# Graph layer and mixture of experts on one core: carries joined two tiles at a time without masks, and a bias add moved from GpSimd to VectorE

## The chip, the cores and the metric

The kernel runs on one core of a Trainium2 chip. The metric is device time in microseconds (us). A core has five engines that each work through their own instructions in order: TensorE (PE in the profile, its weight loads PEld), VectorE (DVE), ScalarE (ACT), GpSimd (POOL) and SyncE (SP). They meet through semaphores. DMA transfers are issued from the queues of SP, of ScalarE and of GpSimd.

## The reference, cut to what matters

There are 6250 nodes with 256 features and 100,000 edges with 96 features. The edges come sorted by `dst`, the node that they end in.

```python
out1 = segment_sum(edge_attr, dst)            # sum of the edges of each node
cnt  = segment_sum(ones, dst)
out2 = where(cnt > 0, segment_max(edge_attr, dst), 0)
out3 = out1 / maximum(cnt, 1)
h = concatenate([xn, out1, out2, out3, u], axis=1)     # xn = layernorm(x)
x = x + relu(h @ W1 + b1) @ W2 + b2 + xn
...
x = x + layernorm(xm + top2_experts(xm)) * gamma + beta   # xm = layernorm(x)
```

The change touches `out1` and `out2`, and the place where `b2` is added. The second layer (16 experts, two for each node) is not touched.

## The kernel before, in words

**Tiles and groups.** The nodes are cut into NT = 50 tiles of P = 125. Groups g0 to g12 take them from the last tile to the first: g0 has 2 tiles, every other group 4. The kernel has an MLP stage (about the first 820 us), which goes through the groups, and then a stage of expert blocks. An edge stream runs inside the MLP stage.

**Edge stream.** For most edges sums and maxima are made by VectorE in `steps` (L299 to L330): edges are cut into runs, and each run is scanned from its end to its start, so that the row of an edge holds the sum and the maximum over the rest of its node's edges in that run. A step for one edge of every run is a pair of instructions of 125x768 elements (L316 and L317, then L319 and L320), with loads (L176) and stores to `rows_d` (L329) through SP's queue. A node whose edges go on past the end of a run needs the rest from the following run. `chain_runs` (L378) works this out for all runs of a region and stores it as rows of `carry_d` (L440, GpSimd's queue). There are seven regions, each of which has to be there before the groups that need it.

**From edges to a group's input.** For groups g2 to g12:
- `index_nodes` (L621), called four times for several groups at once, finds for each node the row of `rows_d` with its first edge (`first_i`) and the row of `carry_d` with its possible carry (`next_i`). The mask `cross` is 1 where the node has a carry and 0 where not; `gate_m` is plus or minus the largest float, from the same mask.
- `take_edges` (L718) and `take_carry` (L726) fetch the rows with indirect DMAs that GpSimd issues, one for each tile.
- `join_edges` (L733) adds the carry times `cross` to the sum (L735), and takes the maximum with the carry cut down by `gate_m` (L737). Both are VectorE instructions of 96 elements, for each tile.
- `mask_edges` (L740, ScalarE) clears nodes without edges and makes the mean. `turn` (L745) transposes on PE and copies on ScalarE.

Groups g0 and g1 get their edges in another way (windows) and have no joins.

**The node's own features.** `take_x` loads `xt`; `stats_x`, `root_x`, `scale_x` find the layernorm. `keep_x` (L709) turns `xt` into x plus its layernorm, with four ScalarE instructions of 256 elements (L714), and then GpSimd adds `b2`, spread over the partitions as `b2b`, to all four tiles in one instruction (L716). When the MLP has its output, `residual` (L782, VectorE) adds it to `xt` (L784) and makes the next statistics. That add also frees the accumulator that the matmuls of the following group use (L766, L771).

**After the MLP.** `norm_b` (L801, ScalarE, L806) writes the normed row `xr`, `turn_b`, `logits`, `choose` (L829), `rank` and `place` (L864) find the two experts, and `send` (L889) stores two rows for each node to `xg_d` with GpSimd's indirect DMAs (L891). `xr` has one buffer, so the next group's `norm_b` waits for these stores.

**The order of the work** is written out by a planner at build time. Each task has a slot; group g begins at slot B = 12 g, and each engine gets its instructions in the order of the tasks. Between one slot and the next the planner puts pieces of the edge stream into VectorE's order, as long as a credit lasts: a slot of a full group gives 4.6 (us, as the planner sees it), a piece (a pair of instructions) takes 1.9, and tasks on VectorE take their own `cost`. What a slot overdraws is missing in the next. If `take_edges` needs a region that isn't finished, the stream is emitted up to it at once (`edges_until`, L1165).

Of group g, `scale_x` is in slot B-10, `take_edges` in B-10 and B-9, `take_carry` in B-9 and B-8, `keep_x` in B-7, the joins of tiles 0 and 1 in B-6 and of tiles 2 and 3 in B-5, `mask_edges` in B-5 and B-4, `residual` in B+9 to B+12. Between them lie those of other groups: in B-9 `norm_b` of group g-2 and `norm_x` of g, in B-8 and B-7 `turn_b` of g-2, in B-5 `choose` of g-2, in B-2 `place` of g-2. (For g2, `keep_x` and the first joins share slot B-4.)

```python
at_slot(B - (4 if g == GW else 7), keep_x, g)
...
for i in range(n if g >= GW else 0):
    at_slot(B - (4 if g == GW else 6) + i // 2, join_edges, g, i, cost=0.6)
    at_slot(B - (4 if g == GW else 5) + i // 2, mask_edges, g, i)
```

Of the kernel before, what the change touches and what calls it, by code (L numbers as in the profile page):

```python
# [9 lines left out]
F32 = mybir.dt.float32  # L10
# [4 lines left out]
OP = mybir.AluOpType  # L15
# [4 lines left out]
P = 125  # L20
PA = 80
RR = 8
GW = 2
WE = 20
WB = 5
JR = (6, 5, 5, 10, 21, 20, 28)
# [13 lines left out]
BIG = 3.4028234663852886e38  # L40
# [4 lines left out]
def kernel(  # L45
# [18 lines left out]
    nc = tc.nc  # L64
    N, D = x.shape
    E, EF = edge.shape
# [3 lines left out]
    NT = N // P  # L70
    EJ = E // P
    EP = P * RR
# [17 lines left out]
    GRP = [(GS * (NG - 1 - g), GS * (NG - 1 - g) + (GS if g else N0)) for g in range(NG)]  # L90
# [5 lines left out]
    dram = ctx.enter_context(tc.tile_pool(name="dram", bufs=1, space=DRAM))  # L96

    rows_d = dram.tile([ER, 2 * EF], F32, name="rows_d")
    carry_d = dram.tile([len(JR) * EP, 2 * EF], F32, name="carry_d")
    xg_d = dram.tile([NE * N, DR], F32, name="xg_d")  # L100
    y_d = dram.tile([NE * N, D], I32, name="y_d")

# [26 lines left out]
    meta = ctx.enter_context(tc.tile_pool(name="meta", bufs=1))  # L129
    ne_n = meta.tile([P, NT], F32, name="ne_n")  # L130
    rc_n = meta.tile([P, NT], F32, name="rc_n")
    cross = meta.tile([P, NT], F32, name="cross")
    gate_m = meta.tile([P, NT], F32, name="gate_m")
    first_i = meta.tile([P, NT], I32, name="first_i")
    next_i = meta.tile([P, NT], I32, name="next_i")
    cnt_f = meta.tile([P, NT], F32, name="cnt_f")
# [14 lines left out]
    b2b = wgt.tile([P, D], F32, name="b2b")  # L151
# [34 lines left out]

    mlp = ExitStack()
    ld = mlp.enter_context(tc.tile_pool(name="ld", bufs=2))
    ga = mlp.enter_context(tc.tile_pool(name="ga", bufs=4))
    wk = mlp.enter_context(tc.tile_pool(name="wk", bufs=2))  # L190
    htp = mlp.enter_context(tc.tile_pool(name="ht", bufs=HC + 1))
    gtp = mlp.enter_context(tc.tile_pool(name="gt", bufs=2))
# [185 lines left out]
    def chain_runs(c):  # L378
        prev = prevs.pop(c)
        ct = chp.tile([P, RR, 2 * EF], F32, name="ct")  # L380
        kb, kp, kb2 = (chp.tile([P, RR], F32, name=nm) for nm in ("kbar", "kp", "kbar2"))

        def over_runs():

            nc.vector.tensor_scalar(kb, kall[:, c], 2.0, -1.0, op0=OP.mult, op1=OP.add)
            nc.vector.tensor_scalar(kb, kb, BIG, None, op0=OP.mult)
            nc.vector.tensor_tensor_scan(kp[:, ::-1], kall[:, c, ::-1], kall[:, c, ::-1], 1.0, op0=OP.mult, op1=OP.min)
            nc.vector.tensor_scalar(kb2, kp, 2.0, -1.0, op0=OP.mult, op1=OP.add)
            nc.vector.tensor_scalar(kb2, kb2, BIG, None, op0=OP.mult)
            run = tuple(a[:, RR - 1, :] for a in prev)  # L390
            for h in range(2):
                nc.scalar.copy(ct[:, RR - 1, h * EF:(h + 1) * EF], run[h])
            for r in reversed(range(RR - 1)):
                to = ct[:, r, 0:EF], ct[:, r, EF:]
                nc.vector.scalar_tensor_tensor(to[0], run[0], kall[:, c, r:r + 1], prev[0][:, r, :], op0=OP.mult, op1=OP.add)
                nc.vector.scalar_tensor_tensor(to[1], run[1], kb[:, r:r + 1], prev[1][:, r, :], op0=OP.min, op1=OP.max)
                run = to
                if r % 3 == 0:
                    yield 1.8
            for_pe(to_features)  # L400

        def to_features():
            over_runs.pk = pk = eps.tile([EF, 3, P], F32, name="ps")
            nc.tensor.transpose(pk[:, 0, :], kp[:, 0:1].to_broadcast([P, EF]), ident[:P, :P])
            for h in range(2):
                nc.tensor.transpose(pk[:, 1 + h, :], ct[:, 0, h * EF:(h + 1) * EF], ident[:P, :P])

        def over_partitions():
            pk = over_runs.pk
            st = chp.tile([EF, 2, P + 1], F32, name="st", bufs=2)  # L410
            for h in range(2):
                if chain[0] is None:
                    nc.vector.memset(st[:, h, P:], 0.0)
                else:
                    nc.vector.tensor_copy(st[:, h, P:], chain[0][:, h, 0:1])
            kk = chp.tile([EF, 2, P], F32, name="kk")
            nc.vector.tensor_copy(kk[:, 0, :], pk[:, 0, :])
            nc.vector.tensor_scalar(kk[:, 1, :], kk[:, 0, :], 2.0, -1.0, op0=OP.mult, op1=OP.add)
            nc.vector.tensor_scalar(kk[:, 1, :], kk[:, 1, :], BIG, None, op0=OP.mult)
            for h in range(2):  # L420
                nc.vector.tensor_tensor_scan(st[:, h, P - 1::-1], kk[:, h, ::-1], pk[:, 1 + h, ::-1], st[:, h, P:],
                                             op0=(OP.mult, OP.min)[h], op1=(OP.add, OP.max)[h])
            chain[0] = st
            yield 2.0
            for_pe(to_partitions)

        def to_partitions():
            over_runs.pc = pc = eps.tile([P, 2 * EF], F32, name="ps")
            for h in range(2):
                nc.tensor.transpose(pc[:, h * EF:(h + 1) * EF], chain[0][:, h, 1:], ident[:EF, :EF])  # L430

        def to_runs():
            tmp = chp.tile([P, RR, EF], F32, name="tmp")
            for h, k, o0, o1 in ((0, kp, OP.mult, OP.add), (1, kb2, OP.min, OP.max)):
                cs = ct[:, :, h * EF:(h + 1) * EF]
                nc.vector.tensor_tensor(tmp, over_runs.pc[:, None, h * EF:(h + 1) * EF].to_broadcast([P, RR, EF]),
                                        k[:, :, None].to_broadcast([P, RR, EF]), op=o0)
                nc.vector.tensor_tensor(cs, cs, tmp, op=o1)
                yield 1.9
            nc.gpsimd.dma_start(carry_d[EP * c:EP * (c + 1)].rearrange("(p r) f -> p r f", p=P), ct)  # L440

        return [over_runs, over_partitions, to_runs]

# [36 lines left out]
    def node_cols(b):  # L480
        g0 = sum(IB[:b])
        return GRP[g0 + IB[b] - 1][0], GRP[g0][1]
# [138 lines left out]
    def index_nodes(b):  # L621
# [31 lines left out]
        nc.vector.tensor_mul(m, q, J)  # L653
        nc.vector.tensor_add(m, m, e0)
        nc.vector.scalar_tensor_tensor(cross[:, cols], end, nf, m, op0=OP.mult, op1=OP.is_gt)
        nc.vector.tensor_scalar(gate_m[:, cols], cross[:, cols], 2.0, -1.0, op0=OP.mult, op1=OP.add)
        nc.vector.tensor_scalar(gate_m[:, cols], gate_m[:, cols], BIG, None, op0=OP.mult)

        nc.vector.tensor_scalar(m, q, float(EP), -2.0 * EP, op0=OP.is_equal, op1=OP.mult)
        nc.vector.tensor_add(q, q, m)  # L660
        nc.vector.tensor_add(q, q, q0)
        nc.vector.tensor_scalar(next_i[:, cols], q, nf, 0.0, op0=OP.mult, op1=OP.max)

        nc.vector.scalar_tensor_tensor(m, e0, -2.0, f, op0=OP.mult, op1=OP.add)
        nc.vector.scalar_tensor_tensor(m, J, float(-EP), m, op0=OP.mult, op1=OP.add)
# [43 lines left out]
    def keep_x(g):  # L709

        n = GRP[g][1] - GRP[g][0]
        xt = G[g]["xt"]
        for i in range(n):
            nc.scalar.activation(xt[:, i, :], xt[:, i, :], AF.Identity, scale=G[g]["rs1"][:, i:i + 1],  # L714
                                 bias=G[g]["nb"][:, i:i + 1])
        nc.gpsimd.tensor_tensor(xt[:, :n], xt[:, :n], b2b[:, None, :].to_broadcast([P, n, D]), op=OP.add)  # L716

    def take_edges(c, g, i):  # L718
        t = GRP[g][0] + i
# [5 lines left out]

    def take_carry(c, g, i):  # L726
        t = GRP[g][0] + i
        cg = ga.tile([P, 2 * EF], F32, name="cg")
        nc.gpsimd.indirect_dma_start(out=cg, out_offset=None, in_=carry_d[0:EP * (c + 1), :],
                                     in_offset=IndirectOffsetOnAxis(ap=next_i[:, t:t + 1], axis=0))  # L730
        G[g].setdefault("cg", []).append(cg)

    def join_edges(g, i):  # L733
        t, gi, cg = GRP[g][0] + i, G[g]["at"][:, i, 0:2 * EF], G[g]["cg"][i]
        nc.vector.scalar_tensor_tensor(gi[:, 0:EF], cg[:, 0:EF], cross[:, t:t + 1], gi[:, 0:EF],  # L735
                                       op0=OP.mult, op1=OP.add)
        nc.vector.scalar_tensor_tensor(gi[:, EF:], cg[:, EF:], gate_m[:, t:t + 1], gi[:, EF:],  # L737
                                       op0=OP.min, op1=OP.max)

    def mask_edges(g, i):  # L740
        t, gi = GRP[g][0] + i, G[g]["at"][:, i, 0:2 * EF]
# [417 lines left out]
    def at_slot(T, fn, *a, cost=0.0):  # L1159
        tasks.append((T, len(tasks), fn, a, cost))  # L1160
# [21 lines left out]
    for g, (a, z) in enumerate(GRP):  # L1182
        B, n = SLOTS * g, z - a
        if g:
# [9 lines left out]
            for i in range(n):  # L1194
# [4 lines left out]
                else:  # L1199
# [4 lines left out]
                    at_slot(2 * i + 2, add_window, g, i, cost=0.9)  # L1204
                    at_slot(2 * i + 2, mask_window, g, i, cost=0.4)
                    at_slot(min(2 * i + 5, SLOTS - 2), mean_window, g, i)
            at_slot(B - (4 if g == GW else 7), keep_x, g)
            for k in range(DC):
                at_slot(B - (4 if g == GW else 6) + k, turn, g, k)
            for i in range(n if g >= GW else 0):  # L1210
                at_slot(B - (4 if g == GW else 6) + i // 2, join_edges, g, i, cost=0.6)
                at_slot(B - (4 if g == GW else 5) + i // 2, mask_edges, g, i)
            for k in range(DC, KC + 1):
                at_slot(B - 3 + k - DC + (1 if g == GW and k < DC + 2 else 0), turn, g, k)
# [73 lines left out]
    def loads_3():  # L1288
        nc.sync.dma_start(b2b, bass.AP(tensor=b2.tensor, offset=b2.offset, ap=[[0, P], [1, D]]))
        nc.sync.dma_start(gws, gate_w.rearrange("(k p) e -> p k e", p=128))  # L1290
        nc.sync.dma_start(gbs, bass.AP(tensor=gate_b.tensor, offset=gate_b.offset, ap=[[0, P], [1, NE]]))
# [79 lines left out]
    with tc.manual_schedule():  # L1371
# [21 lines left out]
        root_x(1)  # L1393
        scale_x(1)
        loads_3()
        for t in reversed(range(*node_cols(GW))):
            find_block(t)
        for k in range(DC):
# [94 lines left out]
```

## Time and profile before

| what | us |
|---|---|
| three runs: lowest, median, highest | 1313.06, 1313.23, 1322.8 |
| the profiled execution, its own time | 1304.08 |
| span of that execution | 1302.3 |
| busy: PE, PEld | 1134.1 (87% of the span), 788.7 (61%) |
| busy: DVE, ACT, POOL | 929.0 (71%), 646.4 (50%), 591.3 (45%) |
| GpSimd's bias add (L716), 12 of 4 tiles | 30.0 |
| joins (L735 and L737), 44 of each | 22.7 and 15.7 |

How to read it: "busy" is the time in which an engine had an instruction at work; times are of one execution, and start points are counted from the start of the span. A group in the profile has its line in the code, its engine and operation, what it writes and reads, and the shape of both, then how often it ran, the busy time, the mean duration in ns, and, after the second bar, the idle time of the engine just before it and what ended that. In a timeline the columns are start, duration, engine, line and the instruction; a bracket at the end holds the idle time before it and its releaser. In the list of waits the columns are the total in us, how often, and the longest. The slices are 40 equal parts of the span, each digit the busy share in tenths, and PEclk the TensorE clock that was granted, in tenths of full speed.

### The profile page before, as it was taken

The numbers are of one execution on the slowest core, as the hardware profiler recorded it, in microseconds if no ns is written. First come the engines' busy times: TensorE is split into PE (matmuls) and PEld (weight loads), VectorE is DVE, ScalarE is ACT, GpSimd is POOL, SyncE is SP. The second block draws the span as 40 slices with busy tenths as digits, with TensorE's granted clock in tenths as the row PEclk, the third lists the DMA queues.
The fourth block names the chain that finished last, engine by engine and source line by source line (L and its number), as shares of the span: only waits on it lengthen the run. The fifth ranks groups of instructions, "written<-read, shape, count | busy, mean of one in ns | idle before, by whom it ended". The sixth has DMA issues, their size and how long they took to land.

```text
span 1302.3 us, 16684 instructions
## 1 busy us (share of the span) xinstructions
PE 1134.1 (87%) x4631; PEld 788.7 (61%) x4631; DVE 929.0 (71%) x2465; ACT 646.4 (50%) x1484; POOL 591.3 (45%) x731
## 2 busy tenths in 40 slices
PE   2494899879888879999999999997999999999992
PEld 1262365536545444646465565886888888888882
DVE  4569888869996989989999441444347767776764
ACT  3394256444637452533435333221266766676663
POOL 4122254563466654383643450303046656555664
PEclk9897799889998989989989999998999999999997
DMA  5948876795888897879988311222366777878771
GB/s 161 217 103 237 212 231 183 202 273 149 237 213 260 230 289 192 245 202 257 262 245 241 105 50 62 65 66 81 120 230 223 257 253 262 278 246 270 268 271 70
DMA packets 179473, 260.99 MB, mean 200 GB/s; under 512 B 35915, under 2 KB 145963, under 8 KB 173729
## 3 DMA queue, kind: packets, MB, share of 16 engines
q1 hardware_dynamic: 140241, 202.11, 52.0%
q0 software_dynamic: 39008, 57.22, 15.5%
q8 instruction: 40, 0.66, 0.2%
q14 instruction: 72, 0.59, 0.1%
q10 hardware_dynamic: 112, 0.41, 0.1%
HBM read 146.59 MB, written 121.88 MB: 206 GB/s over the span
## 4 chain that ended last, share of the span: by engine, by line
PE 30%; DMA 8%; DVE 7%; issue 3%; ACT 3%; SPq 2%; POOL 2%; DVEq 0%; POOLq 0%; ACTq 0%
PE acc L1122 9%; PE acc L1142 9%; PE acc L771 6%; DMA eb<-in_eb_dram 5%; PE acc L779 3%; POOL xg_d L891 1%; DMA xt<-in_x_dram 1%; DVE yb L1053 1%; PE pT L1036 1%; ACT yb L1055 1%; DMA rows_d<-rw 1%; DVE bsc L1079 1%; DMA cg<-carry_d,next_i 1%; DVE z L1089 1%; ACT hb L1128 1%
## 5 line engine op out<-in xcount | busy, mean ns | idle before, releaser
L771 PE MATMUL acc<-inT,w1x 128*128 128x500 f32 (+1 forms) x832 | 374.3, 601 | 0.0
L771 PEld LDWEIGHTS acc<-inT,w1x 128*128 128x128 f32 x832 | 162.7, 203 | 184.1 <-issue 182.2
L891 POOL DMA_INDIRECT xg_d<-xr,pos_i x100 | 133.4, 1334 | 241.1 <-DVE xr L886 177.6
L1122 PE MATMUL acc<-xT,wt 128*128 128x256 f32 x912 | 223.9, 389 | 15.2 <-ACT hb L1128 13.6
L1142 PE MATMUL acc<-wt,hb 128*128 128x256 f32 x912 | 206.8, 380 | 0.0
L1122 PEld LDWEIGHTS acc<-xT,wt 128*128 128x128 f32 x912 | 169.8, 192 | 45.9 <-ACT hb L1128 23.0
L1142 PEld LDWEIGHTS acc<-wt,hb 128*128 128x128 f32 x912 | 173.9, 191 | 23.9
L779 PE MATMUL acc<-w2s,hT 128*125 128x256 f32 x800 | 183.6, 386 | 0.0
L773 ACT ACTIVATE hT<-acc,c 128x500 f32<-128x500 f32 (+1 forms) x104 | 68.5, 658 | 226.2 <-PE acc L771 226.0
L779 PEld LDWEIGHTS acc<-w2s,hT 128*125 128x125 f32 x800 | 150.7, 192 | 22.8 <-issue 0.9
L1096 POOL DMA_INDIRECT out_dram<-g,to_i x86 | 95.7, 1113 | 104.2 <-ACT xT L1039 73.0
L1066 POOL DMA_INDIRECT g<-y_d,from_i x86 | 89.9, 1046 | 88.4 <-DVE to_i L1046 51.8
L495 POOL DMA_INDIRECT gb<-in_dst_dram,blk_i x50 | 67.9, 1359 | 131.1 <-DVE blk_i L492 77.6
L1128 ACT ACTIVATE hb<-acc,wt 128x256 f32<-128x256 f32 x200 | 87.9, 465 | 51.7 <-PE acc L1122 51.7
L1055 ACT ACTIVATE yb<-yb,xb 128x256 f32<-128x256 f32 x114 | 51.7, 501 | 103.1 <-DVE yb L1053 101.7
L316 DVE TENSOR_TENSOR rw<-rw,keep 125x768 f32<-125x768 f32 x81 | 77.2, 953 | 11.3 <-DMA rows_d<-rw 9.8
L319 DVE TENSOR_TENSOR rw<-rw,raw 125x768 f32<-125x768 f32 x88 | 83.4, 948 | 0.3 <-DMA raw<-in_edge_dram 0.3
L320 DVE TENSOR_TENSOR rw<-rw,raw 125x768 f32<-125x768 f32 x88 | 83.6, 950 | 0.0
L317 DVE TENSOR_TENSOR rw<-rw,bar 125x768 f32<-125x768 f32 x81 | 82.1, 1013 | 0.0
L756 ACT COPY inT<-pT 128x500 f32<-128x500 f32 (+1 forms) x65 | 35.9, 553 | 89.6 <-PE pT L755 89.5
L722 POOL DMA_INDIRECT at<-rows_d,first_i x44 | 62.5, 1420 | 37.6 <-issue 19.0
L1041 DVE TENSOR_TENSOR xe<-xb,eb 128x512 f32<-128x512 f32 x57 | 39.4, 691 | 55.7 <-DMA eb<-in_eb_dram 55.7
(301 smaller groups left out, 1633.5 us busy)
## 6 DMA issues: line engine op xcount, KB each, us to landing
wt<-in_wpack_dram SPq DMA_DIRECT2D x44, 1026.0 KB
rows_d<-rw SPq DMA_DIRECT2D x46, 960.0 KB
rows_d<-rw SPq DMA_DIRECT2D x46, 540.0 KB
raw<-in_edge_dram SPq DMA_DIRECT2D x46, 480.0 KB
xb<-xg_d SPq DMA_DIRECT2D x57, 261.0 KB
y_d<-yb SPq DMA_DIRECT2D x57, 256.0 KB
raw<-in_edge_dram SPq DMA_DIRECT2D x46, 270.0 KB
xt<-in_x_dram SPq DMA_DIRECT2D x12, 500.0 KB
```

What stands on the lines that cost most here:

```text
L316: nc.vector.tensor_tensor(su, prev[0], keep[c][:, :, s + j, None].to_broadcast(bcast), op=OP.mult)
L317: nc.vector.tensor_tensor(mx, prev[1], bar[c][:, :, s + j, None].to_broadcast(bcast), op=OP.min)
L319: nc.vector.tensor_tensor(su, su, x_j, op=OP.add)
L320: nc.vector.tensor_tensor(mx, mx, x_j, op=OP.max)
L771: nc.tensor.matmul(pH[:, :n * P], w1x[:, k, ms], inT[:, k, :n * P], start=False, stop=(k == KC - 1))
L779: nc.tensor.matmul(pO, G[g]["hT"][m][:, i * P:(i + 1) * P], w2s[:, m, :], start=(m == 0), stop=(m == HC - 1))
L891: d = nc.gpsimd.indirect_dma_start(out=xg_d[:, :], out_offset=IndirectOffsetOnAxis(ap=G[g]["pos"][:, i, k:k + 1], axis=0), in_=G[g]["xr"][ ...
L1066: d = nc.gpsimd.indirect_dma_start(out=g[:, h, :].bitcast(I32), out_offset=None, in_=y_d[:, :], in_offset=IndirectOffsetOnAxis(ap=BL[b]["f ...
L1096: d = nc.gpsimd.indirect_dma_start(out=out[:, :], out_offset=IndirectOffsetOnAxis(ap=BL[b]["to"][:, h:h + 1], axis=0), in_=g[:, h, :], in_ ...
L1122: nc.tensor.matmul(pB[i][:, half, :], wt[:, k * FF + m * 128:k * FF + (m + 1) * 128], xT[:, k, :], start=(k == 0), stop=(k == DC - 1))
L1128: nc.scalar.activation(hb[:, m, :], pB[i][:, half, :], AF.Relu, bias=bias)
L1142: nc.tensor.matmul(pY[:, h, :], hb[:, m, h * 128:(h + 1) * 128], wt[:, W2O + m * D:W2O + (m + 1) * D], start=(m == order[0]), stop=(m == o ...
```

## The change

- `carry_d` gets one more row in front, row 0, with 0 for the sum and minus the largest float for the maximum. `no_carry` writes it once, near the start, with two VectorE memsets and one transfer in SP's queue. The other rows move up by one.
- `next_i` becomes (q + 1) times `cross`: a node without a carry fetches row 0. `gate_m` and the two instructions that made it go.
- The carries of two tiles share one buffer (`cg`), and `join_edges` works on two tiles at once, with a plain add and a plain maximum of 2 x 96 elements each. It has a cost of 0.8 for two tiles, where it was 0.6 for one. The pool has two such buffers instead of four single ones.
- In `keep_x` the add of `b2b` is a VectorE instruction; the task gets a cost of 1.2.

```diff
-    carry_d = dram.tile([len(JR) * EP, 2 * EF], F32, name="carry_d")
+    carry_d = dram.tile([1 + len(JR) * EP, 2 * EF], F32, name="carry_d")
...
-    ga = mlp.enter_context(tc.tile_pool(name="ga", bufs=4))
+    ga = mlp.enter_context(tc.tile_pool(name="ga", bufs=2))
...
-            nc.gpsimd.dma_start(carry_d[EP * c:EP * (c + 1)].rearrange("(p r) f -> p r f", p=P), ct)
+            nc.gpsimd.dma_start(carry_d[1 + EP * c:1 + EP * (c + 1)].rearrange("(p r) f -> p r f", p=P), ct)
...
-        nc.vector.tensor_scalar(gate_m[:, cols], cross[:, cols], 2.0, -1.0, op0=OP.mult, op1=OP.add)
-        nc.vector.tensor_scalar(gate_m[:, cols], gate_m[:, cols], BIG, None, op0=OP.mult)
...
-        nc.vector.tensor_scalar(next_i[:, cols], q, nf, 0.0, op0=OP.mult, op1=OP.max)
+        nc.vector.scalar_tensor_tensor(next_i[:, cols], q, 1.0, cross[:, cols], op0=OP.add, op1=OP.mult)
...
-        nc.gpsimd.tensor_tensor(xt[:, :n], xt[:, :n], b2b[:, None, :].to_broadcast([P, n, D]), op=OP.add)
+        nc.vector.tensor_tensor(xt[:, :n], xt[:, :n], b2b[:, None, :].to_broadcast([P, n, D]), op=OP.add)
...
     def take_carry(c, g, i):
         t = GRP[g][0] + i
-        cg = ga.tile([P, 2 * EF], F32, name="cg")
-        nc.gpsimd.indirect_dma_start(out=cg, out_offset=None, in_=carry_d[0:EP * (c + 1), :],
+        if i % 2 == 0:
+            G[g].setdefault("cg", []).append(ga.tile([P, 2, 2 * EF], F32, name="cg"))
+        nc.gpsimd.indirect_dma_start(out=G[g]["cg"][i // 2][:, i % 2, :], out_offset=None, in_=carry_d[0:1 + EP * (c + 1), :],
                                      in_offset=IndirectOffsetOnAxis(ap=next_i[:, t:t + 1], axis=0))
-        G[g].setdefault("cg", []).append(cg)
...
     def join_edges(g, i):
-        t, gi, cg = GRP[g][0] + i, G[g]["at"][:, i, 0:2 * EF], G[g]["cg"][i]
-        nc.vector.scalar_tensor_tensor(gi[:, 0:EF], cg[:, 0:EF], cross[:, t:t + 1], gi[:, 0:EF],
-                                       op0=OP.mult, op1=OP.add)
-        nc.vector.scalar_tensor_tensor(gi[:, EF:], cg[:, EF:], gate_m[:, t:t + 1], gi[:, EF:],
-                                       op0=OP.min, op1=OP.max)
+
+        n = min(2, GRP[g][1] - GRP[g][0] - i)
+        gi, cg = G[g]["at"][:, i:i + n], G[g]["cg"][i // 2][:, :n]
+        nc.vector.tensor_tensor(gi[:, :, 0:EF], cg[:, :, 0:EF], gi[:, :, 0:EF], op=OP.add)
+        nc.vector.tensor_tensor(gi[:, :, EF:2 * EF], cg[:, :, EF:], gi[:, :, EF:2 * EF], op=OP.max)
+
+    def no_carry():
+
+        none = chp.tile([P, RR, EF], F32, name="tmp")[0:1, 0:2].rearrange("p h f -> p (h f)")
+        nc.vector.memset(none[:, 0:EF], 0.0)
+        nc.vector.memset(none[:, EF:], -BIG)
+        nc.sync.dma_start(carry_d[0:1, :], none)
...
-            at_slot(B - (4 if g == GW else 7), keep_x, g)
+            at_slot(B - (4 if g == GW else 7), keep_x, g, cost=1.2)
...
             for i in range(n if g >= GW else 0):
-                at_slot(B - (4 if g == GW else 6) + i // 2, join_edges, g, i, cost=0.6)
+                if i % 2 == 0:
+                    at_slot(B - (4 if g == GW else 6) + i // 2, join_edges, g, i, cost=0.8)
                 at_slot(B - (4 if g == GW else 5) + i // 2, mask_edges, g, i)
...
         loads_3()
+        no_carry()
```

More of the change, by code (lines that the diff above doesn't have):

```diff
@@ L132 @@
     cross = meta.tile([P, NT], F32, name="cross")
-    gate_m = meta.tile([P, NT], F32, name="gate_m")
     first_i = meta.tile([P, NT], I32, name="first_i")
```

## The prediction

> **What bounds the kernel now.** I read the page's 40 slices first, then the list of waits, then the groups of VectorE and GpSimd by shape, then the timelines of the engines around each edited instruction.
>
> ```profile
> PE   2494899879888879999999999997999999999992
> DVE  4569888869996989989999441444347767776764
> POOL 4122254563466654383643450303046656555664
> PEclk9897799889998989989989999998999999999997
> ```
>
> A slice is 32.6 us. Slices 5 to 22 (about 130 to 725 us) are the MLP stage with the edge stream; there PE and DVE are both near full, and neither is alone the bound. After 725 us the edge stream is over, DVE drops to 1 to 4 tenths and PE sets the time. So the edit counts in the groups of tiles g2 to g11; in g12 and in the expert blocks it touches nothing that binds.
>
> ```profile
> POOL xt L716 <- ACT xt L714: 42.3, 6, 23.8
> DVE at L735 <- DMA cg<-carry_d,next_i: 37.7, 10, 10.3
> PE acc L766 <- DVE xt L784: 8.8, 5, 2.6
> ```
>
> Three facts: GpSimd's bias add was in 6 of 13 cases ready before ScalarE's scaling (L714) was; VectorE lost 37.7 us in front of joins, waiting for carry rows; and the matmuls wait for VectorE's residual add (L784), but only 8.8 us in all, so a faster VectorE has a limited reward.
>
> **The change, part by part** (in steps of issue: back to back, the next instruction starts about 0.08 us before the printed end; a 0.95 us instruction of 768 elements repeats every 0.87).
>
> ```profile
> L735 DVE SCALAR_TENSOR_TENSOR at<-cg,cross,at 125x96 f32<-125x96 f32 x44 | 22.7, 515 | 37.7 <-DMA cg<-carry_d,next_i 37.7
> L737 DVE SCALAR_TENSOR_TENSOR at<-cg,gate_m,at 125x96 f32<-125x96 f32 x44 | 15.7, 357 | 0.0
> L582 DVE TENSOR_TENSOR w<-w 125x960 f32<-125x960 f32 x6 | 6.9, 1158 | 0.2
> L582 DVE TENSOR_TENSOR w<-w 125x192 f32<-125x192 f32 x6 | 2.1, 357 | 0.2
> ```
>
> *Joins.* Of the four masked instructions of two tiles each takes 0.31 us in the timeline and repeats every 0.23: 0.92 us a pair of tiles. (The means 515 and 357 are pulled up by a few stretched ones; see below.) After: two plain TENSOR_TENSOR of 192 elements, 0.357 us each by the last row, 0.277 to issue: 0.55. Gain 0.36 a pair, 20 pairs in g2 to g11: **-7.2 us** of VectorE.
>
> *Bias add.* No row has 1024 elements; between 480 (658 ns) and 960 (1158) the slope is 1.04 ns, so 1.225 us, 1.145 to issue. Eleven of them, g1 to g11: **+12.6**. The adds of g0 (before the stage) and g12 lie in VectorE's idle time.
>
> *Index arithmetic.* Two gate_m instructions (0.17 each) go in four calls; next_i keeps its one: **-1.4**.
>
> *The neutral row.* Two memsets of 96 elements and one 768 B transfer on SP's queue near 37 us. SP waits there for VectorE; behind it in the queue stand the w2s load and the first edge loads, which wait for the same windows to be cut anyway. 0; without that cover the two memsets, under 0.3 us.
>
> *What GpSimd's add did to VectorE.*
>
> ```profile
> L716 POOL TENSOR_TENSOR xt<-xt,b2b 125x1024 f32<-125x1024 f32 x12 | 30.0, 2502 | 18.6 <-ACT xt L714 18.5
> ```
> ```profile
> 339.78 0.95 DVE L316 TENSOR_TENSOR rw<-rw,keep 125x768 f32<-125x768 f32 x1
> 340.65 3.50 DVE L317 TENSOR_TENSOR rw<-rw,bar 125x768 f32<-125x768 f32 x1
> 344.07 0.95 DVE L319 TENSOR_TENSOR rw<-rw,raw 125x768 f32<-125x768 f32 x1
> ```
> ```profile
> 340.95 2.37 POOL L716 TENSOR_TENSOR xt<-xt,b2b 125x1024 f32<-125x1024 f32 x1
> ```
>
> L317 usually takes 0.95; this one took 3.50 because GpSimd's add ran from 340.95 to 343.32. The same stretch is there in every group: the excess over the usual duration is about 2.2 (g1), 0 (g2), 0.3 (g3), 1.6, 2.6, 1.0, 3.2, 2.6, 2.1, 2.1, 2.1 (g11): **-19.7 us** of VectorE when the add leaves GpSimd. Here a rule of the Trainium skill stands behind the row. "SBUF — State Buffer" (SBUF: two separate sides) says that VectorE with two SBUF inputs and GpSimd hold a shared port pair as an exclusive lock for a whole instruction. By the rule alone I would take off up to 2.37 us in each of 11 groups, 26; but in g2 VectorE was then reading PSUM or one input and lost nothing, and in g3 it was mostly idle. I take the rows, 19.7.
>
> A second page speaks against the edit: "Perfetto Trace Analysis" (Identifying Performance Opportunities) has one find the most contended engine and relieve it. VectorE is that engine here, and by its own instruction count the edit loads it: +12.6 - 7.2 - 1.4 = +4.0, which would give slower by 4. With the stretches the sum is 4.0 - 19.7 = -15.7. That is VectorE's work, not yet its time.
>
> *The new wait.* VectorE works in order. The add is issued in slot B-7, right after ScalarE's four scalings (L714), and VectorE now stands until they are done. Behind it stand the stream instructions of one slot, then the first two joins of slot B-6, then the residual adds that free the accumulators for PE. How many stream pieces lie between? Nine pairs of 0.87 us instructions lie between scale_x (B-10) and the join in g10 and g11; with a credit of 4.6 a slot and 1.9 a pair, the split over four slots leaves two pairs after the add for most starting credits, three for the rest. I take two (3.48 us).
>
> ```profile
> 695.99 0.95 DVE L319 TENSOR_TENSOR rw<-rw,raw 125x768 f32<-125x768 f32 x1
> 696.86 0.95 DVE L320 TENSOR_TENSOR rw<-rw,raw 125x768 f32<-125x768 f32 x1
> 700.36 0.96 DVE L316 TENSOR_TENSOR rw<-rw,keep 125x768 f32<-125x768 f32 x1 [2.55 <-DMA rows_d<-rw]
> 701.23 0.95 DVE L317 TENSOR_TENSOR rw<-rw,bar 125x768 f32<-125x768 f32 x1
> 702.10 0.31 DVE L735 SCALAR_TENSOR_TENSOR at<-cg,cross,at 125x96 f32<-125x96 f32 x1
> 702.33 2.41 DVE L737 SCALAR_TENSOR_TENSOR at<-cg,gate_m,at 125x96 f32<-125x96 f32 x1
> ```
> ```profile
> 692.25 2.93 ACT L806 ACTIVATE xr<-xt,stat 125x512 f32<-125x512 f32 x4 [4.01 <-DMA cg<-carry_d,next_i]
> 699.99 2.08 ACT L714 ACTIVATE xt<-xt,nba,rs 125x256 f32<-125x256 f32 x4
> ```
>
> In g11 VectorE would arrive at 695.99 and ScalarE ends at 702.07: 6.1 us of standing. Then 1.15 add, 3.48 stream, 0.55 joins: 707.25, where before the pair of joins was over at 705.12 (it had lost 2.55 to a store of rows and 2.1 to the stretch). So +2.1. The same for each group (arrival, L714's end, pair over before, pair over after):
> g3: 217.7, 216.2, 224.7, 224.0: -0.7 (the wait for a store, to 221.7, stays)
> g4: idle till the carry anyway, 286.0, 290.8, 289.5: -1.3
> g5: 339.8, 338.5, 346.7, 345.0: -1.8
> g6: 394.2, 407.7, next stream at 410.8, now 413.5: +2.7 (the stream pairs that ran ahead of the idle time now come after it)
> g7: 467.2, 473.9, 478.65, 479.1: +0.4
> g8: 529.4, 530.1, 536.4, 535.3: -1.1
> g9: 586.7, 590.2, 593.3, 595.4: +2.1
> g10: 643.0, 644.9, 649.5, 650.05: +0.6
> g11: +2.1. In g2 the add stands directly before the joins (slot B-4): +0.25.
> Together +3.3. Second pairs of g3 to g11, 9 x 0.36: -3.3. Index: -1.4. g1: 1.15 for 2.2, of which I count half as on the path: -0.6. **Sum -2.0 us.** Against the profiled execution: 1304.1 (span 1302.3, 1.8 around it) becomes 1302.1. The three runs shown have 1313.2 as median, 9 us above the profiled one; the same step gives **1311 us**.
>
> GpSimd loses 31 us of work and 42 us of waiting, but what follows the add in its queue (sends, block gathers, carry stores) waits for VectorE (177.6 us in front of L891), so nothing is gained there.
>
> *Not in the trace:* about a sixth of the gathers' rows (from the spread of dst) now read row 0 together. Carry gathers land after 3.5 to 9.8 us, median 8.5. If the common row pushed each to 9.8, the joins that wait for carries in g2, g4, g6, g7 would each lose 1.3, together 5; if it makes them as quick as 7.4 (the edge gathers' median), -4. I take 0, as the same queue and packet size serve both; the ends go into the range.
>
> **Rivals.**
> *Cover holds (20%).* If VectorE mostly comes to the add after ScalarE, the -15.7 is earned. For: in g3, g5 it does already. Against: g6, g7, g9, g11. PE's waits for VectorE cap it: 8.8 (L766 on L784) and 3.8 (L860 on L851), 12.6. So -12.6 to -15.7: about 1299.
> *The wait takes over the loop (17%), slower.* Place: the ring from PE's restart after a residual, over ScalarE's L714, over the add to the next residual. Restart to L714's end took 30.2, 29.6 and 32.6 us in g9, g10, g11 (560.05 to 590.20, 615.32 to 644.87, 669.47 to 702.07). Add 1.15. From the add to the residual, g10 had 26.5; less 2.1 of stretch and 0.7 of joins, 23.7. With 32.6 the ring is 57.4 against 54.9 before: +2.5 in six groups, g6 to g11, +15: 1328. It decides from a ScalarE end 30 us after the restart; below that there is no loss. For: g11. Against: g9 and g10 lie at the line.
> *Nothing moves (inside the likeliest).* PE waits little for VectorE, and its own work fills most of a period: 1313.
>
> **How the numbers follow.** Likeliest 55% (its own range 1304 to 1319: three stream pairs instead of two in the seven groups that wait would add 12, two of them are likely to), cover 20%, ring 17%, the rest, 8%, spread to both sides (the common row, order of transfers). Range for 8 in 10: 1300 to 1325. A measurement of this kernel can tell about 1% (13 us) from no change. Faster than 1300: four fifths of the second case and a little of the rest, 0.17. Slower than 1326: the ring's case and a little, 0.18. Same: 0.65.
>
> **What would show it.** After: no stretched VectorE instruction beside a GpSimd add; a new row "DVE xt L713 waits for ACT xt L714" (the add's line) of some 15 to 25 us in g6 to g11; joins of 0.36 us x44; VectorE's busy time lower by about 15 us with the idle time higher by as much; restarts of PE still 54 to 57 us apart. It is wrong if that new wait is near 0 (cover) or over 3 us in every group with restarts over 57 us apart (ring); or if the joins' wait for carry rows grows, which would be the common row.

## The result and the profile after

| kernel | runs | lowest, median, highest (us) | profiled execution |
|---|---|---|---|
| before | 4 | 1307.27, 1313.14, 1322.8 | span 1302.3 |
| after | 4 | 1339.4, 1354.66, 1363.42 | span 1357.6 |

The changed kernel takes 1.0281 times as long (95% interval 1.0229 to 1.0334): slower, by more than the rival on the slow side had named. The run of 1363.42 us counts as slow (over 1.5% above the fastest) and is left out of this ratio. Nearly everything that the prediction said of single instructions is in the trace; the time is not where it said. (Lines of the changed kernel: scaling L711, VectorE's add L713, joins L734 and L735, stream pairs L315/L316 and L318/L319, edge load L175 and store of rows L328, carry store L439 and its gathers L727, chain over runs from L384, with ScalarE's copy into `ct` in L391, residual L788, `norm_b` L810, `place` to L890, `send` L895. In the kernels of the experiments they shift by a few.)

The slices of the page after, 34 us each:

```profile
PE   2595695969987878999899999997999999999992
DVE  4579685959884877898888740444336767666665
POOL 4121243372627283535606332303036656555564
PEclk9896897979988889989898999999999999999997
```

In the seventh slice (204 to 238 us) PE and VectorE fall to 5, where a 9 and an 8 stood; in the ninth and the thirteenth (271 to 305 and 407 to 441 us) VectorE shows 5 and 4. VectorE's groups by shape (busy us, mean ns of one | idle us before it, and for what):

```profile
L316 DVE TENSOR_TENSOR rw<-rw,bar 125x768 f32<-125x768 f32 x81 | 77.0, 951 | 0.0
...
L713 DVE TENSOR_TENSOR xt<-xt,b2b 125x1024 f32<-125x1024 f32 x12 | 14.7, 1225 | 77.3 <-ACT xt L711 60.9 <-issue 16.4
...
L734 DVE TENSOR_TENSOR at<-cg,at 125x192 f32<-125x192 f32 x22 | 7.8, 353 | 13.9 <-DMA cg<-carry_d,next_i 10.1 <-issue 3.7
L735 DVE TENSOR_TENSOR at<-cg,at 125x192 f32<-125x192 f32 x22 | 7.7, 351 | 0.0
```

The joins take 0.35 us, the add 1.225, as worked out; the mean of 0.951 on L316 says that no stream instruction is stretched any more. VectorE is busy 911.0 us instead of 929.0. But in front of the add it stands for 77 us. In g6 to g11, for which the prediction had named 15 to 25 us, it is 36.4. In g11, shown before, the standing is small:

```profile
740.73 0.95 DVE L319 TENSOR_TENSOR rw<-rw,raw 125x768 f32<-125x768 f32 x1
744.71 1.23 DVE L713 TENSOR_TENSOR xt<-xt,b2b 125x1024 f32<-125x1024 f32 x1 [3.02 <-ACT xt L711]
745.85 0.95 DVE L315 TENSOR_TENSOR rw<-rw,keep 125x768 f32<-125x768 f32 x1
746.72 0.95 DVE L316 TENSOR_TENSOR rw<-rw,bar 125x768 f32<-125x768 f32 x1
747.59 0.95 DVE L318 TENSOR_TENSOR rw<-rw,raw 125x768 f32<-125x768 f32 x1
748.45 0.95 DVE L319 TENSOR_TENSOR rw<-rw,raw 125x768 f32<-125x768 f32 x1
749.32 0.35 DVE L734 TENSOR_TENSOR at<-cg,at 125x192 f32<-125x192 f32 x1
```

Two stream pairs behind the add, then the join: the prediction's picture. Where the loss is, the timeline of PE tells: the start of each group's first hidden matmul in the two traces, in us. (The prediction's restarts are up to 4 us later, where PE goes on after its wait for the residual.)

| group | g2 | g3 | g4 | g5 | g6 | g7 | g8 | g9 | g10 | g11 | g12 |
|---|---|---|---|---|---|---|---|---|---|---|---|
| before | 188.4 | 242.5 | 310.2 | 368.4 | 430.4 | 497.4 | 556.7 | 612.9 | 667.7 | 724.8 | 774.4 |
| after | 193.6 | 263.1 | 330.9 | 394.7 | 465.9 | 537.5 | 596.1 | 651.8 | 710.4 | 768.1 | 819.9 |
| later by | 5.2 | 20.6 | 20.7 | 26.3 | 35.5 | 40.1 | 39.4 | 38.9 | 42.7 | 43.3 | 45.5 |

Forty of the 45 us are lost by g7; I had looked for the danger in g6 to g11. (Another 9.8 us of this execution lie behind the start of g12. That stretch took 526.0 to 536.9 us in the experiments' kernels, 527.9 before and 537.7 here, and no cause was looked for.) The largest single step, 15 us, is between g2 and g3. There the changed kernel shows, in the queues of SP and GpSimd and on VectorE, ScalarE and PE:

```profile
207.85 1.55 SPq L175 DMA_DIRECT2D raw<-in_edge_dram  x2
209.44 1.60 SPq L328 DMA_DIRECT2D rows_d<-rw  x2
```
```profile
212.23 0.60 POOL L439 DMA_DIRECT2D carry_d<-ct  x1 [16.11 <-DMA raw<-in_edge_dram]
...
226.14 1.21 POOL L727 DMA_INDIRECT cg<-carry_d,next_i  x1 [9.24 <-DMA carry_d<-ct]
```
```profile
215.93 0.17 DVE L388 TENSOR_SCALAR kbar<-kbar 125x8 f32<-125x8 f32 x1
225.88 0.32 DVE L394 SCALAR_TENSOR_TENSOR ct<-rw,kall 125x96 f32<-125x96 f32 x1 [9.78 <-DMA carry_d<-ct]
```
```profile
225.93 0.45 ACT L391 COPY ct<-rw 125x96 f32<-125x96 f32 x2 [18.94 <-DMA carry_d<-ct]
226.28 0.67 ACT L777 ACTIVATE hT<-acc,c 128x500 f32<-128x500 f32 x1
226.85 2.92 ACT L810 ACTIVATE xr<-xt,stat 125x512 f32<-125x512 f32 x4
```
```profile
227.71 0.47 PE L822 MATMUL pT<-ident,xr 125*128 125x125 f32 x1 [14.09 <-ACT xr L810]
```

And the kernel before at the same place, on SP, GpSimd, ScalarE and VectorE:

```profile
207.72 1.55 SPq L176 DMA_DIRECT2D raw<-in_edge_dram  x2
209.32 1.60 SPq L329 DMA_DIRECT2D rows_d<-rw  x2
```
```profile
204.52 0.59 POOL L440 DMA_DIRECT2D carry_d<-ct  x1 [13.14 <-DVE ct L438]
```
```profile
205.22 2.92 ACT L806 ACTIVATE xr<-xt,stat 125x512 f32<-125x512 f32 x4
...
210.82 0.65 ACT L392 COPY ct<-rw 125x96 f32<-125x96 f32 x2
```
```profile
212.00 0.31 DVE L395 SCALAR_TENSOR_TENSOR ct<-rw,kall 125x96 f32<-125x96 f32 x1
```

An "x2" of SP's queue is two transfers: loads of 480 and 270 KB, stores of 960 and 540 KB. Before, the second region's carry store (750 KB) was issued 3.2 us ahead of the first of these loads, and landed after 5.3 us. After, it was issued 4.4 us behind that load, and its readers were released at 225.9, 13.7 us later. VectorE's next chain over runs writes the one `ct` buffer that the store reads, so it stood 9.8 us; ScalarE stood 18.9 in front of its copy into `ct` (13.7 of it after the store's issue); and PE stood 14.1 for `norm_b`, which ScalarE has behind that copy. None of these engines waits there for the add or the joins. What has changed is the order. Between the end of `to_runs` (which ends with the carry store) and the next chain stand four stream instructions where there were eight; and ScalarE's copy, a part of that chain, has moved with it from behind `norm_b` to ahead of it.

That order comes from two numbers of the diff that my prediction passed over: the planner is told that `keep_x` costs 1.2 (it cost nothing) and a pair of joins 0.8 (1.2 before). They change no instruction, only what the credit leaves for stream pieces in each slot.

At that seam PE lost more than its pause. From 213.6 to 227.7 us it stood; the granted clock was 0.50 for the first 5.8 us after that, and 1.00 again from 233.5. Before, it was 1.00 from 213 to 233. From the start of g2 to that of g7 (309.0 us before, 343.9 after) PE's idle time grew from 41.8 to 68.1 us, and its busy time, for as many matmuls, from 267.2 to 275.8, at a mean granted clock of 0.93 and 0.89. So some 9 of the 35 us lost there are a slower PE. That the pauses bring the lower clock is likely by the times, but no run tests it.

### The profile page after: what moved, and what is told of

It is laid out like the page before. It is cut to its first block, busy times and chain, and to the rows that moved or that the text cites. A ratio compares the mean times of both kernels' runs of the same rounds, so it can differ in the third digit from the quotient of the medians.

```text
span 1357.6 us, 16595 instructions
## 1 busy us (share of the span) xinstructions
PE 1146.5 (84%) x4631; PEld 793.1 (58%) x4631; DVE 911.0 (67%) x2428; ACT 645.8 (48%) x1484; POOL 569.2 (42%) x718
## 4 chain that ended last, share of the span: by engine, by line
PE 41%; DVE 19%; DMA 16%; ACT 7%; issue 7%; POOL 3%; SPq 2%; another core or an unknown queue 0%; DVEq 0%; POOLq 0%; ACTq 0%
PE acc L775 14%; PE acc L1146 11%; PE acc L1126 11%; DMA xt<-in_x_dram 3%; DMA rows_d<-rw 3%; DVE rw L319 2%; DVE rw L316 2%; DMA eb<-in_eb_dram 2%; PE acc L783 2%; DVE rw L318 2%; DMA cg<-carry_d,next_i 2%; DMA xg_d<-xr,pos_i 2%; DVE rw L315 2%; PE acc L770 2%; DMA raw<-in_edge_dram 1%
## 5 line engine op out<-in xcount | busy, mean ns | idle before, releaser
L775 PE MATMUL acc<-inT,w1x 128*128 128x500 f32 (+1 forms) x832 | 379.9, 608 | 0.0
L895 POOL DMA_INDIRECT xg_d<-xr,pos_i x100 | 131.6, 1316 | 287.4 <-issue 144.5
L777 ACT ACTIVATE hT<-acc,c 128x500 f32<-128x500 f32 (+1 forms) x104 | 68.5, 658 | 237.1 <-PE acc L775 224.9
L494 POOL DMA_INDIRECT gb<-in_dst_dram,blk_i x50 | 74.4, 1488 | 175.9 <-DVE blk_i L491 65.0
L319 DVE TENSOR_TENSOR rw<-rw,raw 125x768 f32<-125x768 f32 x88 | 83.7, 951 | 0.0
L318 DVE TENSOR_TENSOR rw<-rw,raw 125x768 f32<-125x768 f32 x88 | 83.6, 950 | 0.0
L315 DVE TENSOR_TENSOR rw<-rw,keep 125x768 f32<-125x768 f32 x81 | 76.8, 948 | 10.1 <-DMA rows_d<-rw 10.1
L1057 DVE TENSOR_TENSOR yb<-acc,xe 128x512 f32<-128x512 f32 x57 | 39.3, 690 | 65.0 <-PE acc L1146 56.3
L727 POOL DMA_INDIRECT cg<-carry_d,next_i x44 | 70.0, 1590 | 27.7 <-issue 12.2
```

Source lines behind the costliest of these rows:

```text
L315: nc.vector.tensor_tensor(su, prev[0], keep[c][:, :, s + j, None].to_broadcast(bcast), op=OP.mult)
L318: nc.vector.tensor_tensor(su, su, x_j, op=OP.add)
L319: nc.vector.tensor_tensor(mx, mx, x_j, op=OP.max)
L494: nc.gpsimd.indirect_dma_start(out=gbs_[t], out_offset=None, in_=dst_b, in_offset=IndirectOffsetOnAxis(ap=blk_i[:, t:t + 1], axis=0))
L775: nc.tensor.matmul(pH[:, :n * P], w1x[:, k, ms], inT[:, k, :n * P], start=False, stop=(k == KC - 1))
L895: d = nc.gpsimd.indirect_dma_start(out=xg_d[:, :], out_offset=IndirectOffsetOnAxis(ap=G[g]["pos"][:, i, k:k + 1], axis=0), in_=G[g]["xr"][ ...
```

## The experiments

Ratios are to the kernel before on the same chip, with the 95% interval. Its median was 1301.78 us beside `order_kept`, `costs_only`, `joins_only` and `add_only`; 1310.78 beside `add_late`, `add_mid` and `more_cost`; 1309.94 beside `scale_early`, `scale_pool`, `costs_mid` and `mid_j08`; and 1306.24 beside `seam_only`.

**The two parts of the change and its costs.** `order_kept` is the changed kernel with the costs of before. Its VectorE order is then that of before but for the changed instructions.

```diff
-            at_slot(B - (4 if g == GW else 7), keep_x, g, cost=1.2)
+            at_slot(B - (4 if g == GW else 7), keep_x, g)
-                    at_slot(B - (4 if g == GW else 6) + i // 2, join_edges, g, i, cost=0.8)
+                    at_slot(B - (4 if g == GW else 6) + i // 2, join_edges, g, i, cost=1.2)
```


> All of the change, with the planner's costs as before it (no cost for the scaling with its add, 1.2 for a pair of joins), so that VectorE's instructions stand in the order of before. Order theory (the new costs moved pieces of the edge chain, and the carry store then holds up VectorE, ScalarE and PE in g3 and g6): 1310 to 1322 us, restart of g3 back at about 247 to 252 us instead of 264.6. Wait theory (VectorE stands in order in front of the add, in every group): 1345 to 1355, g3 still at 260 or later. Common-row theory (a sixth of the carry gathers read one row): 1345 to 1355 too.

1.0121 (1.0082 to 1.0161), 1319.97 us; g3 starts at 245.7. Both theories are half right: the order takes away the jump at g3, and over 1% stays.

`costs_only` is the kernel before with the new costs, nothing else:

```diff
-            at_slot(B - (4 if g == GW else 7), keep_x, g)
+            at_slot(B - (4 if g == GW else 7), keep_x, g, cost=1.2)
-                at_slot(B - (4 if g == GW else 6) + i // 2, join_edges, g, i, cost=0.6)
+                at_slot(B - (4 if g == GW else 6) + i // 2, join_edges, g, i, cost=0.8 if i % 2 == 0 else 0.0)
```


> The instructions of before, in the order that the change's costs give (1.2 for the scaling, 0.8 for two joins instead of 1.2); GpSimd still adds the bias and the joins are masked. Order theory: 1340 to 1355 us, with VectorE waiting some 10 us for the carry store in g3. Wait theory and common-row theory: 1308 to 1316, the time of before.

1.0164 (1.0126 to 1.0203), 1322.79 us, with 7.7 us of VectorE and 17.3 of ScalarE for the carry store in g3. Two numbers of the planner, with every instruction as before, make the kernel slower by 1.6%. That is well below the 1340 us at least that the order theory had named: the order is one part of the loss, not all of it.

`joins_only` is `order_kept` with the add on GpSimd; `add_only` is the kernel before with only the add moved, at no cost:

```diff
-        nc.gpsimd.tensor_tensor(xt[:, :n], xt[:, :n], b2b[:, None, :].to_broadcast([P, n, D]), op=OP.add)
+        nc.vector.tensor_tensor(xt[:, :n], xt[:, :n], b2b[:, None, :].to_broadcast([P, n, D]), op=OP.add)
```


> The neutral row and the joins of two tiles, in the order of before, with the bias add left on GpSimd. Order theory and wait theory: 1304 to 1314 us (some of the 8.6 us that VectorE saves). Common-row theory: 1345 to 1355, with longer waits for carry rows.

> The kernel before with nothing but the bias add moved to VectorE, at no cost to the planner, so in the order of before. Order theory: 1312 to 1322 us. Wait theory: 1345 to 1355, or somewhat more, since the joins stay long. Common-row theory: 1310 to 1316.

`joins_only`: 1.0009 (0.998 to 1.0038), 1304.14 us. The joins and the neutral row gain nothing and cost nothing; the common-row theory falls. `add_only`: 1.0139 (1.01 to 1.0177), 1319.26 us. The add in slot B-7 costs over 1% although VectorE's stretches are gone (0.951 us for an instruction of L317, 1.013 before).

**The standing in front of the add.** Two kernels take the add away from the scaling: it becomes a task of its own, in B-3 (`add_late`) or B+2 (`add_mid`), in the order of before. Against `order_kept`, for `add_mid`:

```diff
-        nc.vector.tensor_tensor(xt[:, :n], xt[:, :n], b2b[:, None, :].to_broadcast([P, n, D]), op=OP.add)
+
+    def add_bias(g):
+
+        n = GRP[g][1] - GRP[g][0]
+        xt = G[g]["xt"]
+        nc.vector.tensor_tensor(xt[:, :n], xt[:, :n], b2b[:, None, :].to_broadcast([P, n, D]), op=OP.add)
...
+            at_slot(B + 2, add_bias, g)
```


> All of the change in the order of before, but with VectorE's add as a task of its own four slots after the scaling (B-3 in place of B-7), behind the joins, at no cost to the planner. Wait theory (VectorE stands in order for a scaling that ScalarE has not finished): the standing goes, the stretches beside GpSimd stay gone, so 1288 to 1302 us against 1302 for the kernel before. Work theory (the add loads VectorE, wherever it stands): 1312 to 1320, as with the add at B-7.

> The same, with the add still later, in slot B+2 amid the hidden matmuls of its own group, seven slots before the residual that reads it. Wait theory: 1288 to 1302, within 5 us of the add at B-3. Work theory: 1312 to 1320.

`add_late`: 1.0051 (1.002 to 1.0081), 1317.99 us; `add_mid`: 1.0004 (0.9985 to 1.0023), 1312.81 us. The same add that costs 1.2% in B-7 costs nothing in B+2: it is the standing, not the work. But the gain that I expected once it was gone is not there either. Why the add in B-3 keeps half a per cent was not followed up.

How does the standing (0.1 to 14.2 us in g2 to g12 of `order_kept`) reach PE? One lap there, from `place` of g8 to the add of g11, on VectorE, GpSimd and ScalarE:

```profile
681.89 0.17 DVE L890 SCALAR_TENSOR_TENSOR xr<-i,posf 125x8 f32<-125x8 f32 x1
...
713.08 0.95 DVE L316 TENSOR_TENSOR rw<-rw,bar 125x768 f32<-125x768 f32 x1
722.31 1.23 DVE L713 TENSOR_TENSOR xt<-xt,b2b 125x1024 f32<-125x1024 f32 x1 [8.27 <-ACT xt L711]
```
```profile
682.98 1.21 POOL L895 DMA_INDIRECT xg_d<-xr,pos_i  x1 [29.56 <-issue]
...
694.83 1.43 POOL L895 DMA_INDIRECT xg_d<-xr,pos_i  x1 [0.22 <-issue]
```
```profile
709.57 2.93 ACT L810 ACTIVATE xr<-xt,stat 125x512 f32<-125x512 f32 x4 [6.84 <-DMA at<-rows_d,first_i]
...
720.20 2.08 ACT L711 ACTIVATE xt<-xt,nba,rs 125x256 f32<-125x256 f32 x4
```

`place` ends on VectorE at 682.1; then GpSimd issues eight sends out of the one `xr` buffer, to 696.3; ScalarE's `norm_b` wants that buffer and starts at 709.6 (the profile names a gather of the same queue as the releaser, but the last of the eight sends landed at 709.4, by the updates of its semaphore); the scaling is behind `norm_b` on ScalarE and ends at 722.3; VectorE waits for it, and with it its stream pieces, joins, `choose` and the next `place`, at 743.4. One lap took 61.3 us here, 53.7 in `add_mid` (671.9 to 725.6). If this ring is the cause, the scaling must be taken out of it. `scale_early` leaves the add in B-7 and puts normalization and scaling of g3 and later ahead of `norm_b` in ScalarE's order; `scale_pool` is the same with the add on GpSimd. Against `order_kept`, for `scale_early`:

```diff
-            at_slot(B - 9 + (4 if g == GW else 0), norm_x, g)
+            at_slot(B - 9 + (4 if g == GW else 0) - (0.5 if g > GW else 0), norm_x, g)
-            at_slot(B - (4 if g == GW else 7), keep_x, g)
+            at_slot(B - (4 if g == GW else 9.5 if g > GW else 7), keep_x, g)
+            at_slot(B - (4 if g == GW else 7), add_bias, g)
```


> All of the change in the order of before, with VectorE's add at its place of the change (B-7), but ScalarE's scaling (and the normalization before it) ahead of the normalized rows of the group before last in ScalarE's order, for g3 and later. Ring theory (place, sends out of the single xr buffer, ScalarE's wait for that buffer, the scaling behind it, VectorE standing in front of the add, and so the next place late): the standing in g3 to g11 falls from 54 to under 15 us, and the time from 1.2% above the kernel before to within 0.5% of it or below. Rival (the order of VectorE and the work of the add decide, not what ScalarE does before its scaling): still 1.0 to 1.4% above.

> The same early scaling and order, with the add on GpSimd again at its place of before (B-7). Tells what the early scaling does by itself. Ring theory: VectorE never stood for the scaling here, so no more than 0.5% from the kernel before. If the early scaling helps ScalarE and PE by itself: 0.5 to 1.5% faster.

`scale_early`: 1.0031 (1.0004 to 1.0059), 1315.84 us; `scale_pool`: 1.001 (0.9978 to 1.0042), 1309.85 us. VectorE's waits for the scaling in `order_kept` and in `scale_early` (us, times, longest), and its joins in both:

```profile
DVE xt L713 <- ACT xt L711: 69.8, 10, 14.2
```
```profile
DVE xt L718 <- ACT xt L711: 6.3, 2, 4.9
```
```profile
L734 DVE TENSOR_TENSOR at<-cg,at 125x192 f32<-125x192 f32 x22 | 7.8, 353 | 4.0 <-DMA cg<-carry_d,next_i 4.0
```
```profile
L739 DVE TENSOR_TENSOR at<-cg,at 125x192 f32<-125x192 f32 x22 | 7.8, 354 | 45.4 <-issue 20.1 <-DMA cg<-carry_d,next_i 16.0 <-DMA at<-rows_d,first_i 9.3
```

69.8 us of standing became 6.3, at the same place of the add, and about three quarters of the loss went; `scale_pool` says that the early scaling is no gain in itself. So the standing behind `norm_b` is what costs. It is not all new idle time: in front of the joins VectorE stood 41 us longer in `scale_early` than in `order_kept` (37.7 us in the kernel before), so the two together fell by 22 us only.

That the standing grows by coming round the ring is argued, not shown. The link through `xr` is real in about half of the laps: in `order_kept` `norm_b` of g2, g4, g5, g6 and g9 starts within 0.4 us of the landing of the last send, in the other groups from g3 to g11 2.6 us or more after it; but in the kernel before it is the same five groups. A second `xr` buffer would test the ring by itself; it was not tried.

**The order.** `more_cost` charges still more than the change (1.8 and 1.2), which by chance puts eight stream instructions back between carry store and chain.

```diff
-            at_slot(B - (4 if g == GW else 7), keep_x, g, cost=1.2)
+            at_slot(B - (4 if g == GW else 7), keep_x, g, cost=1.8)
-                    at_slot(B - (4 if g == GW else 6) + i // 2, join_edges, g, i, cost=0.8)
+                    at_slot(B - (4 if g == GW else 6) + i // 2, join_edges, g, i, cost=1.2)
```


> The changed kernel with dearer entries for the planner: 1.8 for the scaling with its add and 1.2 for a pair of joins, in place of 1.2 and 0.8. In the resulting order eight edge-stream instructions stand again between the carry store of the second region and the next chain over runs, as before the change; in the changed kernel there are four. Carry-store theory (with four, the one buffer that the store reads is wanted by the next chain before the store has landed): VectorE's wait at the chain falls from 9.8 to about 2 us, and the time to 1318 to 1335. Charge theory (the more is charged for the add, the later the edge stream and all that waits for it): 1355 or more.

1.0246 (1.02 to 1.0292), 1343.02 us. A half miss: the wait at the chain in g3 is gone, and g3 starts 54.6 us after g2 instead of 69.5. But g5 comes 68.5 us after g4 (58.2 before), through the other reader of a carry store:

```profile
337.53 0.60 POOL L439 DMA_DIRECT2D carry_d<-ct  x1 [10.37 <-ACT gT L823]
...
349.46 5.38 POOL L727 DMA_INDIRECT cg<-carry_d,next_i  x1 [7.91 <-DMA carry_d<-ct]
```
```profile
362.24 0.36 DVE L734 TENSOR_TENSOR at<-cg,at 125x192 f32<-125x192 f32 x1 [8.47 <-DMA cg<-carry_d,next_i]
```

The gathers of carries cannot start before the store has landed, here 12 us after its issue, and the joins wait for them. Each order has its own seam.

`costs_mid` keeps the order of the change and moves only the add to B+2; `mid_j08` is `add_mid` with 0.8 for a pair of joins in place of 1.2, which leaves eight instructions at the seam.

> The changed kernel, its planner's costs kept (so VectorE's order of the change), with nothing but the add moved from B-7 to B+2. If the loss is two separate parts, the standing (1.2%) and the order from the costs (1.6%): 1.012 to 1.02 of the time before, with VectorE's wait for the carry store in g3 still about 8 to 10 us. If the two need each other: below 1.008. If the standing alone is what the order makes worse: 1.02 or more.

> The add in slot B+2 at no cost, and 0.8 charged for a pair of joins in place of 1.2; eight edge-stream instructions stand between the second region's carry store and the next chain, and 28 in place of 20 in the third region. Carry-store theory: no longer wait at that chain than in the kernel before (2 to 4 us), so 0.990 to 1.004 of it; any charge that differs from before is harmful: 1.01 or more.

`costs_mid`: 1.0149 (1.0093 to 1.0205), with 9.0 us at the chain. Without its standing the changed kernel is as slow as `costs_only`: the two losses are separate, and 1.0121 x 1.0164 = 1.0287 is what the whole change shows (1.0281). `mid_j08`: 1.0026 (0.9994 to 1.0059): a changed cost alone is not harmful.

`seam_only` tests this seam by itself: it is `add_mid`, with `to_runs` of the second region held back by four stream instructions.

```diff
-        parts, of = [], 0
+        parts, of, held = [], 0, []
...
             if whole and parts and ready():
-                yield from next_part()
+                if of == 1 and len(parts) == 1 and not held:
+                    held.append(of)
+                else:
+                    yield from next_part()
```


> The kernel with the add in slot B+2, costs and order of before, but the spreading of the second region's carry (to_runs) held back by four edge-stream instructions, so that four in place of eight stand between its carry store and the next chain over runs; the order of later regions shifts a little with it. Carry-store theory: the store then starts beside a 960 KB store of rows and lands after 11 to 14 us instead of 5; VectorE waits 7 to 10 us for it at the chain, PE's restart of g3 comes 66 to 70 us after that of g2 instead of 53.6, and the time is 0.7 to 1.5% over that of the kernel before. If the cost of the new order lies elsewhere: g3 after 53 to 56 us, and within 0.4%.

1.0157 (1.0122 to 1.0192), 1326.68 us; g3 starts 68.9 us after g2 (53.6 in `add_mid`). The store, and the waits from 195 to 275 us:

```profile
carry_d<-ct POOLq DMA_DIRECT2D x1, 750.0 KB, 12.7
```
```profile
ACT ct L394 <- DMA carry_d<-ct: 19.4, 1, 19.4
...
PE pT L830 <- ACT xr L818: 15.0, 3, 14.5
...
DVE ct L397 <- DMA carry_d<-ct: 8.9, 1, 8.9
```

Landing, waits and the step of 15 us are those of the changed kernel. ScalarE's copy into `ct` stands ahead of `norm_b` here too, so the late store and the copy's place are tested together, not each alone. The held piece also shifts later regions a little, so the share of the total that this one seam explains is read from the step, not from the ratio. A second `ct` buffer would test it more directly; it was not tried.

No kernel here beats the one before.

## Why the prediction was wrong, step by step

- *Joins, add, index, stretches:* right in size. VectorE's busy time fell by 18.0 us against 15.7. The one wrong size is the new standing in g6 to g11, named as 15 to 25 us, though the rows of the prediction's own table add up to 32. Of the two rules of the Trainium skill that were weighed, the lock of "SBUF — State Buffer" (SBUF: two separate sides) agrees with the trace, where VectorE's work fell; the +4 that went with the rule of "Perfetto Trace Analysis" (Identifying Performance Opportunities) does not, though that page's side, slower, is where the time went.
- *VectorE's work is worth time:* only -2 of it was counted, and even that is not there. `joins_only` (1.0009) and `add_mid` (1.0004) each take work from VectorE; idle time in front of the joins grows instead, to 41.7 and 51.1 us against 37.7 in the kernel before. (The profile puts only 17.8 and 24.3 of it down to carry rows; for the rest it shows no releaser.)
- *The new wait, +3.3:* this step failed. The standing itself was about as the table had it, 36.5 us in g6 to g11 of `order_kept` against its 32. Its price was not: the table charged it only with the delay of the first joins, with VectorE's arrivals and ScalarE's ends as in the trace of before. Measured: +1.2% by `order_kept` against nothing by `add_mid`, some 15 us. Those times are not fixed. From the first hidden matmul of the group before to the end of the scaling, for g8 to g11, `order_kept` took 32.7, 38.1, 32.7 and 39.2 us, `add_mid` 33.7, 37.5, 28.2 and 33.2, the kernel before 32.7, 33.5, 32.0 and 34.4. So against `add_mid` the scaling comes 4.5 and 6.0 us later in g10 and g11, as a ring over `place`, the sends, the single `xr` buffer, `norm_b` and the scaling would make it; in `add_only`, with nearly the same loss, it took 32.7, 36.8, 32.0 and 33.7, which does not show it. How the standing reaches PE in each group stays open. The ring rival named +15, and the number was good, but in part by luck: its ring was a shorter one, from PE's restart to the scaling, and I gave it 17%.
- *The planner's costs:* this step failed too; they were put at nothing. I used the credit to count stream pairs behind the add and never asked what a changed cost moves. It moved the carry store of the second region behind SP's transfers and the next chain, with ScalarE's copy, closer to it by four instructions, and cost 1.5 to 1.6% (`costs_only`, `costs_mid`), some 20 us.
- *The common row:* rightly taken as 0.
- *What would show it wrong:* "over 3 us in every group with restarts over 57 us apart" came near: the standing was 2.2 to 18.2 us in g2 to g12. But that mark could not tell the two causes apart; the start of g3 did.

## What to carry to other kernels

In a kernel whose order is written by a planner, an edit of a cost is an edit of the program: list which pieces change places, above all those that end in a store whose buffer has one copy, and what DMA they then meet. When work moves to an in-order engine, follow what is queued behind it until the chain comes back to the instruction it waits for; if it comes back, the waits of the old trace need not be the waits of the new one. Place such work in a slot where its input has long been ready: here the same add cost 1.2% in one slot and nothing nine slots later.

## What the runs showed of the hardware that was not expected

The landing of one 750 KB store depends on its place among the others by more than its own length: 5.3 us when issued 3.2 us ahead of 750 KB of loads and 1500 KB of stores in SP's queue, 12.7 (`seam_only`) and 13.7 us when issued 4.4 us behind the first of them.

The stretch between GpSimd and VectorE also goes the other way. In `joins_only` a GpSimd add took twice its usual 2.37 us beside VectorE:

```profile
645.40 4.53 POOL L713 TENSOR_TENSOR xt<-xt,b2b 125x1024 f32<-125x1024 f32 x1 [7.15 <-ACT xt L711]
```
```profile
647.37 0.35 DVE L735 TENSOR_TENSOR at<-cg,at 125x192 f32<-125x192 f32 x1
648.41 2.33 DVE L315 TENSOR_TENSOR rw<-rw,keep 125x768 f32<-125x768 f32 x1 [0.69 <-DMA rows_d<-rw]
```

VectorE ran back to back at full speed until it paused at 647.7; GpSimd's add ended at 649.9, 2.2 us later, and now VectorE's next instruction was the stretched one. The kernel before has a case as well: its add of g10, from 644.96, took 3.77 us beside two stream instructions of 0.95 each, and the join behind them, with no pause between, took 2.41. What decides which of the two engines waits was not tested.
